# A block-sparse layer with a LoRA gate on one core: mask products a tile later, the second query ahead of a weight product, fills and mask products of the folds in other places

## The chip, the core and the metric

The kernel runs on one core of one Trainium2 chip. A core has five engines with a queue of instructions each: TensorE (PE in the profile; its weight loads are listed as PEld), VectorE (DVE), ScalarE (ACT), GpSimd (POOL) and SyncE (SP), which here issues loads and stores. Engines work side by side and meet at semaphores. Transfers between the chip's memory (HBM) and the core's SBUF are asked for by SP, ACT or POOL and carried by 16 DMA engines. Sums of matmuls are gathered in PSUM. The metric is the device time of one launch in microseconds (us); each kernel is run several times and the median is given.

## What is computed

```python
x  = L0_attn_data                              # [2, 1024, 1024]
xn = layernorm(x)
bm = mask.reshape(32, 32, 32, 32).sum(axis=(1, 3)) > 0     # 32 x 32 blocks
s  = einsum('bsk,nk->bsn', xn, weight * blocks(bm)) + bias
q      = einsum('bi,ki->bk', xn.mean(axis=1), Wq)
coeffs = softmax(einsum('bk,ek->be', q, keys) / sqrt(128))  # 8 experts
y  = xn @ W_org.T + einsum('be,bser,ero->bso', coeffs, xn @ lora_down, lora_up)
out = x + s * silu(y)
```

Everything is float32. The query q of a batch gives eight coefficients, so the gate's weights differ between the two batches: for each batch the kernel adds the scaled product of lora_down and lora_up into W_org once ("folding") and then multiplies by the sum.

## The kernel before

Each float32 operand is kept as two parts, a high part (a cast, on ScalarE) and a low part (what the cast lost, a subtraction on VectorE); a product is three matmuls, high by high, high by low, low by high. One tile of the output is 128 rows by 512 columns, summed over eight slices of 128 (`kt`), so 24 matmuls (lines 450, 453, 454). All of batch 0 is done in this way, in four stages of eight tiles (S and gate, two column halves each). Batch 1 runs after it in eight "units" of a Strassen scheme (line 1213), with seven sums of x for each slice group (`fill`, lines 1051 to 1063) and seven sums of weights (`unit_mask`, `unit_sum`, `unit_split`).

The order on TensorE, VectorE, ScalarE and GpSimd is that in which the program issues: the whole kernel is inside a manual schedule for these four. Only SP's order is the compiler's scheduler's.

The stages that the change touches:

- **Phase b** (`phase("y", 0, 0, y00, True, jobs_b)`, line 970 on). Eight tiles of batch 0's gate, each followed by one fold of the next weight half, `mix_jobs` (lines 873 to 883): `y_prep` loads a slice of lora_down (`ds`) and one of W_org (`wo`) and splits `ds` into `dhi` (ScalarE, L405) and `dlo` (VectorE, L406); `y_mul` is twelve matmuls into `psw` (L414 to L416); `y_sum` adds `psw` to `wo` on VectorE (L421). Before each tile `flush` issues what was put off: the sum of the last fold, the evacuation of the last tile, the low part. After the fold come the jobs of `jobs_b`. Among them are the block masks of quarters 2 and 3. A mask quarter is loaded in two parts; ScalarE sums each (L251); `mask_spread` makes a small operand `r` on VectorE (L261); `mask_apply_mm` is eight small matmuls with the constant `expand` (L271); `mask_apply_cp` copies the result into `m_sb` on VectorE (L278). `expand` lies in the first third of a buffer `misc`, which later takes loads of lora_up and of the x sums. Behind tile 3 `spread_stats` also turns batch 1's means and reciprocal deviations into rows: a transpose on TensorE (L927), a copy on ScalarE (L929), a store to HBM and two loads broadcast to all partitions on POOL's queue (L930, L934). `wide_a` and `wide_b` (lines 960 to 990) then normalize slices of x with these rows on VectorE (L962, L963) and form the sums (L968), which are stored to HBM.
- **Phase c** (`jobs_c`, line 997 on). Eight tiles of batch 0's gate, second half. Beside them `s_mul` (lines 295 to 303) loads a slice of the S weight, multiplies it by the mask on VectorE (L299) and casts it on ScalarE (L302), `s_lo` makes the low part (L307). Behind tile 5 stand the sums of batch 1's x (`steps[0]`, eight transposes, L322) and its query (`steps[1]`: two products with Wq on VectorE, L346, and `qb`, L350); in the middle of tile 6 stand the scores (`steps[2]`, a matmul that takes `qb`, L357); behind it the softmax and the scaling of lora_up.
- **The folds of batch 1** (lines 1132 to 1149). Five tiles of batch 0's second S half, with 4, 4, 3, 3 and 2 of the 16 folds behind them, and three more tiles after the folds. A fold n first issues `y_prep` of fold n+1, then the store of the last sum (`yu`, from ScalarE's queue), then the twelve matmuls, then the sum. Between folds stand the fills (a load of one x sum into one of three turns of `misc`, a cast on ScalarE, L1062, and a subtraction on VectorE, L1063) and the first six jobs of the first unit (`early`): two mask products of 1024 columns (L1091) and four sums of 512 (L1099). After fold 7 lora_up is scaled for the second half (`scale_up(1, 1, homes)`), with three of its four loads going into `misc`, in the turn behind the fills so far (L389, casts L392, low parts L393).

Of the kernel before, what the change touches and what calls it, by code (L numbers as in the profile page):

```python
# [32 lines left out]
def kernel(  # L33
# [99 lines left out]
    def nat_tile(dt=F32):  # L133
        k = turns[0] % 3
        turns[0] += 1
        v = raw_flat[:, k * D : (k + 1) * D]
        return v if dt == F32 else v.bitcast(dt)
# [107 lines left out]
    def mask_sum(qr, c, mt, eng, part=0):  # L245

        if qr not in msum:
            msum[qr] = small.tile([P, 2, 2], F32, name="s2")
        o = msum[qr][:, part, c : c + 1]
        if eng is nc.scalar:  # L250
            nc.scalar.activation(mt.bitcast(F32), mt, AF.Copy, accum_out=o)  # L251
        else:
            nc.vector.tensor_reduce(o, mt, AX.X, ALU.add)
# [5 lines left out]
    def mask_spread(qr):  # L259
        r4 = small.tile([P, 2, 4], BF16, name="r4")  # L260
        nc.vector.scalar_tensor_tensor(  # L261
            r4, msum[qr][:, 0, :].unsqueeze(2).to_broadcast([P, 2, 4]), 0.0,
            pick4.unsqueeze(1).to_broadcast([P, 2, 4]), ALU.is_gt, ALU.mult,
        )
        spread[qr] = r4

    def mask_apply_mm(qr):
        r4 = spread[qr]
        mp = ps_s.tile([P, NKT, 8], F32, name="mp", tag="ps_s")
        for kt in range(NKT):  # L270
            nc.tensor.matmul(  # L271
                mp[:, kt, :], lhsT=expand[:, kt * P : (kt + 1) * P],
                rhs=r4.rearrange("p a b -> p (a b)"), start=True, stop=True,
            )
        spread[qr] = mp

    def mask_apply_cp(qr):
        nc.vector.tensor_copy(m_sb[:, :, 8 * qr : 8 * (qr + 1)], spread[qr])  # L278

    def mask_part(qr, c, mt=None):  # L280
        if mt is None:
            mt = nat_tile(I32)
        else:
            mt = stage_l.tile([P, D], I32, name="mt", tag="ac", bufs=1)
        nc.sync.dma_start(mt, mask[2 * qr + c])
        mask_sum(qr, c, mt, nc.scalar)
        if c == 1:
            mask_spread(qr)
            mask_apply_mm(qr)
            mask_apply_cp(qr)  # L290

    def new_slot():
        return wpool.tile([P, NKT, 2, NH], F32R, name="slot", tag="w")
# [257 lines left out]
    J = lambda f, *a: (lambda: f(*a))  # L551
# [98 lines left out]
    with tc.manual_schedule(engines={mybir.EngineType.PE, mybir.EngineType.DVE, mybir.EngineType.Activation, mybir.EngineType.Pool}):  # L650
# [237 lines left out]
        def jobs_b(i):  # L888
            if i == 0:
                yield J(scale_up, 0, 1)  # L890
            yield J(mix_jobs, y01, 0, 1, i)
            yield J(store_out, 1)
            if i < 3:
                yield J(act_stats, 1 + i)
            for t in ((4,), (5, 6), (7,), (), (), (), (), ())[i]:
                yield J(nat_stats, t)
            yield from {
                2: [J(mask_part, 2, 0)], 3: [J(mask_part, 2, 1), J(spread_stats), J(mask_part, 3, 0, 1)],
                4: [J(mask_part, 3, 1, 1)],
            }.get(i, ())  # L900
            if i == 3:
                yield J(wide_load, 0, 0)
            if i == 4:
                yield J(wide_load, 0, 1)
                yield J(wide_a, 0)
            if i == 5:
                yield J(wide_b, 0)
                yield J(wide_load, 1, 0)
            if i == 6:
                yield J(wide_a, 1)  # L910
            if i == 7:
                yield J(wide_load, 1, 1)
# [63 lines left out]
        def wide_b(j):  # L976
# [12 lines left out]
            store_sums()  # L989

        phase("y", 0, 0, y00, True, jobs_b)


        s1 = new_slot()
        steps = coeffs(1)

        def jobs_c(i):
            if i < 2:
                yield J(store_out, 1 - i)

            if i < 6:
                yield J(s_mul, s1, 1, i)
            if i == 5:
                yield steps[0]
                yield steps[1]
            if i == 6:
                yield steps[3]
                yield J(scale_up, 1, 0, up_homes)
            if i == 5:
                yield J(s_mul, s1, 1, 6)  # L1010
                yield J(s_mul, s1, 1, 7)
                for kt in (5, 6, 7):
                    yield J(s_lo, s1, 1, kt)
            if i in (0, 2):
                yield J(wide_load, 2 + i // 2, 0)
                yield J(wide_load, 2 + i // 2, 1)
            if i < 5:
                yield J((wide_b, wide_a)[i % 2], 1 + (i + 1) // 2)
                yield J(s_lo, s1, 1, i)

        up_homes = [misc[:, 0, :]]
        split_at[(0, 1, 6)] = steps[2]
        phase("y", 0, 1, y01, False, jobs_c)


        folds = [(h, kt) for h in range(2) for kt in range(NKT)]

        def fold(n):
            h, kt = folds[n]
            if n + 1 < len(folds):  # L1030
                y_prep(1, *folds[n + 1])
            store_late()
            y_mul(1, h, kt)
            flush()
            y_sum(1, h, kt)
            ps, ws = staged.pop((1, h, kt))
            late_stores.append((
                yu[:, :, 2 * h + kt // 4, kt % 4, :].rearrange("u p n -> p u n"),
                ws.rearrange("p (u n) -> p u n", n=P),
            ))  # L1040
            if n == NKT - 1:
                homes = [misc[:, (len(spare) + k) % 3, :] for k in range(3)]
                spare.extend(homes)
                scale_up(1, 1, homes)
# [23 lines left out]
        def s_tile(i):  # L1068
            store_out()
            flush()  # L1070
            ps = gemm(0, i, s1)
            pending.append(J(final_evac, "s", 0, 1, i, ps))
# [6 lines left out]
        def unit_load(u, i):  # L1079
            kind, p = units[u]  # L1080
            src = wu[p] if kind == "s" else yu[p].rearrange("p a j n -> p (a j n)")
            c = slice(2 * i * NH, 2 * (i + 1) * NH)
            nc.sync.dma_start(raw_flat[:, c], src[:, c])
# [45 lines left out]
        def fills(j, n):  # L1129
            for _ in range(n):  # L1130
                fill(j, ORDER_X[filled[j]])
                filled[j] += 1

        for i, n in enumerate((4, 4, 3, 3, 2)):
            s_tile(i)
            for k in range(n):
                fold(done)
                done += 1
                if i < 3 and (i == 2 or k in (1, 2)):
                    fills(0, 1)  # L1140
                if i > 2 and (i == 4 or k):
                    fills(1, 1)
                if i in (2, 3):
                    early.pop(0)()
            if i == 0:
                unit_load(0, 0)
                unit_load(0, 1)
# [219 lines left out]
```

## Time and profile before

| what | value |
|---|---|
| median of 3 runs | 451.43 us (451.36 to 451.67) |
| the profiled execution, its own time | 452.2 us |
| its span, first to last instruction | 450.5 us |
| granted TensorE clock | 0.999 |
| TensorE busy | 440.4 us (98%) |
| VectorE busy | 288.9 us (64%) |
| ScalarE busy | 175.7 us (39%) |
| mean traffic to and from HBM | 200 GB/s |

The profile is one execution. Its page gives busy time by engine, the span in 40 slices, the chain of work that ended last, and the costliest groups of instructions. The trace behind it can be asked for the waits of an engine (who waited for whom, us in total, times, longest), for a timeline (start in us from the span's start, duration, engine, line, operation, output <- inputs, times, and in brackets the idle time of the engine before it with what ended it) and for more. A matmul of 512 columns is listed with 0.39 us because its end is modelled and it overlaps the next one; the distance between two starts, 0.227 us, is what it takes.

### The profile page before, as it was taken

Reading aid. Unit: us, or ns where it says so; the run is one execution under the profiler, and the core shown is the slowest. Engines: PE = TensorE matmul, PEld = TensorE weight load, DVE = VectorE, ACT = ScalarE, POOL = GpSimd, SP = SyncE. Lnnn points to the kernel's source line nnn. Section 1 sums busy time; section 2 is a strip of 40 time slices with the busy share of each in tenths; the row PEclk is TensorE's granted clock in tenths of the full one; section 3 lists DMA queues with packets and bytes.
Section 4 is the critical chain, followed back from the end, with each engine's and each line's share of the span. In section 5 each row is a group of like instructions: output and inputs, shape, how many; then the busy total and the mean of one; then the engine's idle time right before and its main releaser. Section 6 shows DMA issues by size and latency. Waiting matters only on the chain.

```text
span 450.5 us, 5791 instructions
## 1 busy us (share of the span) xinstructions
PE 440.4 (98%) x2058; PEld 363.7 (81%) x2058; DVE 288.9 (64%) x478; ACT 175.7 (39%) x291; POOL 76.4 (17%) x93
## 2 busy tenths in 40 slices
PE   8999999999999999999999999999999999999996
PEld 6789888888878888878887788887888888888885
DVE  6989777766627778864466667487456294365625
ACT  4676535454731222233233135067344322441520
POOL 3774210002220313120000000110020030002000
PEclk9999999999999999999999999999999999999999
DMA  8995306677896889896978987865183146218103
GB/s 280 391 353 198 134 25 210 235 240 224 252 291 184 262 259 331 275 346 192 283 211 284 317 244 226 244 178 187 39 187 140 47 112 170 93 23 218 42 1 116
DMA packets 47741, 90.58 MB, mean 201 GB/s; under 512 B 4816, under 2 KB 15328, under 8 KB 47712
## 3 DMA queue, kind: packets, MB, share of 16 engines
q1 hardware_dynamic: 30624, 66.08, 43.7%
q0 software_dynamic: 6624, 16.26, 15.5%
q10 hardware_dynamic: 10464, 7.87, 5.3%
q8 instruction: 16, 0.26, 0.2%
q14 instruction: 13, 0.11, 0.1%
HBM read 70.26 MB, written 19.93 MB: 200 GB/s over the span
## 4 chain that ended last, share of the span: by engine, by line
PE 68%; DVE 11%; DMA 11%; issue 6%; ACT 3%; POOL 1%; SPq 0%; ACTq 0%; DVEq 0%; POOLq 0%
PE acc_ps L1213 25%; PE py L1213 10%; PE acc_ps L454 7%; PE acc_ps L450 7%; PE acc_ps L453 7%; PE psw L416 4%; PE psw L414 4%; PE psw L415 4%; DMA ws<-in_wT_dram 3%; DMA stash<-in_x_dram 2%; DMA yu<-wo 2%; DVE st L145 1%; DVE slot L591 1%; DMA raw<-in_x_dram 1%; DMA raw<-in_mask_dram 1%
## 5 line engine op out<-in xcount | busy, mean ns | idle before, releaser
L1213 PE MATMUL acc_ps<-xw,ow 128*128 128x512 f32 (+1 forms) x492 | 113.3, 387 | 0.0
L1213 PEld LDWEIGHTS acc_ps<-xw,ow 128*128 128x128 f32 x492 | 91.0, 188 | 19.8 <-ACT acc_ps L1273 0.4
L450 PE MATMUL acc_ps<-slot,xgrp 128*128 128x512 f32 (+1 forms) x288 | 106.5, 370 | 0.1
L454 PE MATMUL acc_ps<-slot,xgrp 128*128 128x512 f32 (+1 forms) x288 | 105.7, 367 | 0.7 <-DVE xgrp L603 0.7
L453 PE MATMUL acc_ps<-slot,xgrp 128*128 128x512 f32 (+1 forms) x288 | 105.7, 367 | 0.6 <-DVE slot L591 0.4
L453 PEld LDWEIGHTS acc_ps<-slot,xgrp 128*128 128x128 f32 x288 | 54.4, 189 | 10.7 <-DVE slot L591 2.1
L454 PEld LDWEIGHTS acc_ps<-slot,xgrp 128*128 128x128 f32 x288 | 54.2, 188 | 10.2 <-DVE xgrp L603 1.1
L450 PEld LDWEIGHTS acc_ps<-slot,xgrp 128*128 128x128 f32 x288 | 54.3, 188 | 9.1 <-DVE stash L466 0.3
L416 PE MATMUL psw<-cut,dlo 128*128 128x512 f32 x128 | 50.0, 390 | 1.2 <-DVE dlo L406 1.2
L414 PE MATMUL psw<-cut,dhi 128*128 128x512 f32 x128 | 50.0, 390 | 0.0
L415 PE MATMUL psw<-cut,dhi 128*128 128x512 f32 x128 | 49.8, 389 | 0.0
L1213 PE MATMUL py<-xw,ow 128*128 128x512 f32 x192 | 46.8, 392 | 0.0
L1213 PEld LDWEIGHTS py<-xw,ow 128*128 128x128 f32 x192 | 36.1, 188 | 7.9
L1106 DVE TENSOR_TENSOR ow<-raw,ow 128x1024 fp32r<-128x1024 f32 (+1 forms) x32 | 34.5, 1088 | 10.9 <-ACT ow L1105 10.9
L405 ACT CAST dhi<-ds 128x512 fp32r<-128x512 f32 x32 | 19.7, 617 | 39.3 <-DMA ds<-in_down_dram 17.0
L502 POOL DMA_DIRECT2D stash<-in_x_dram x16 | 14.4, 898 | 121.5 <-DVE stash L499 121.5
L421 DVE TENSOR_TENSOR wo<-wo,psw 128x512 f32<-128x512 f32 x32 | 21.9, 685 | 16.3 <-PE psw L416 16.0
L1105 ACT CAST ow<-raw 128x1024 fp32r<-128x1024 f32 (+1 forms) x32 | 29.4, 941 | 2.2 <-DVE wo L421 1.6
L416 PEld LDWEIGHTS psw<-cut,dlo 128*128 128x128 f32 x128 | 24.0, 188 | 6.6 <-DVE dlo L406 1.6
L414 PEld LDWEIGHTS psw<-cut,dhi 128*128 128x128 f32 x128 | 24.0, 188 | 5.3 <-ACT dhi L405 0.4
L415 PEld LDWEIGHTS psw<-cut,dhi 128*128 128x128 f32 x128 | 24.1, 188 | 5.0
L1196 POOL DMA_DIRECT2D gate<-in_xT_dram x12 | 10.5, 909 | 94.2 <-DVE gate L1190 68.8
(180 smaller groups left out, 480.5 us busy)
## 6 DMA issues: line engine op xcount, KB each, us to landing
ds<-in_down_dram SPq DMA_DIRECT2D x32, 256.0 KB, 3.6
wo<-in_worgT_dram SPq DMA_DIRECT2D x32, 256.0 KB, 3.8
raw<-in_x_dram SPq DMA_DIRECT2D x11, 512.0 KB, 4.8
stash<-in_x_dram POOLq DMA_DIRECT2D x16, 256.0 KB, 5.2
raw<-in_wu_dram SPq DMA_DIRECT2D x8, 512.0 KB, 4.9
yu<-wo ACTq DMA_DIRECT2D x16, 256.0 KB, 4.9
raw<-yu SPq DMA_DIRECT2D x8, 512.0 KB, 3.6
out_dram<-stash ACTq DMA_DIRECT2D x14, 256.0 KB, 3.9
```

The costliest lines, as they stand in the source:

```text
L405: nc.scalar.copy(dhi, ds)
L414: nc.tensor.matmul(ps, lhsT=dhi[:, c, :], rhs=u[c][:, 0, :], start=c == 0, stop=False)
L415: nc.tensor.matmul(ps, lhsT=dhi[:, c, :], rhs=u[c][:, 1, :], start=False, stop=False)
L416: nc.tensor.matmul(ps, lhsT=dlo[:, c, :], rhs=u[c][:, 0, :], start=False, stop=c == 3)
L421: nc.vector.tensor_tensor(ws, ws, ps, ALU.add)
L450: nc.tensor.matmul(ps, lhsT=xs[:, kt, 0, cols], rhs=w[:, kt, 0, wc], start=kt == 0, stop=False)
L453: nc.tensor.matmul(ps, lhsT=xs[:, kt, 0, cols], rhs=w[:, kt, 1, wc], start=False, stop=False)
L454: nc.tensor.matmul(ps, lhsT=xs[:, kt, 1, cols], rhs=w[:, kt, 0, wc], start=False, stop=kt == NKT - 1)
L502: nc.gpsimd.dma_start(res, x[at], accum_op=ALU.add)
L1105: nc.scalar.copy(o[:, a:b, 0], raw[:, a:b])
L1106: nc.vector.tensor_tensor(o[:, a:b, 1], raw[:, a:b], o[:, a:b, 0].bitcast(F32), ALU.subtract)
L1213: nc.tensor.matmul(ps, lhsT=o[:, a, wl, j, :], rhs=xw[j][:, m, xl, cols], start=start and j == 0 and k == 0, stop=j == 3 and k == 2, skip_ ...
```

## The change

Three edits, none of which adds or drops an instruction. The line numbers of the profile are those of the kernel before; from line 290 on, those of the changed kernel are one higher.

1. The masks of quarters 2 and 3 are no longer spread, multiplied and copied right behind the issue of their second load. `mask_apply` does it one tile later: quarter 2 behind tile 4 (ahead of the second load of quarter 3), quarter 3 behind tile 5.
2. In phase c, behind tile 5, the sums and the query of batch 1 are issued ahead of the sixth S weight's `s_mul`, not behind it.
3. In the folds of batch 1 the fills of the first tile of x move from folds 1, 2, 5, 6, 8, 9, 10 (counted from 0) to folds 1, 2, 3, 4, 5, 9, 10; the mask products and sums of the first unit move from folds 8 to 13 to folds 8, 11, 12, 13, 14, 15. The turns of `misc` that lora_up takes after fold 7 follow the number of fills so far, which is now five and was four.

On SP the scheduler puts the first S weight's load ahead of a lora_up load, and the loads of x sums and lora_up between the folds in the new order.

```diff
@@ mask_part @@
         nc.sync.dma_start(mt, mask[2 * qr + c])
         mask_sum(qr, c, mt, nc.scalar)
-        if c == 1:
-            mask_spread(qr)
-            mask_apply_mm(qr)
-            mask_apply_cp(qr)
+
+    def mask_apply(qr):
+        mask_spread(qr)
+        mask_apply_mm(qr)
+        mask_apply_cp(qr)
@@ jobs_b @@
                 2: [J(mask_part, 2, 0)], 3: [J(mask_part, 2, 1), J(spread_stats), J(mask_part, 3, 0, 1)],
-                4: [J(mask_part, 3, 1, 1)],
+                4: [J(mask_apply, 2), J(mask_part, 3, 1, 1)], 5: [J(mask_apply, 3)],
             }.get(i, ())
@@ jobs_c @@
-            if i < 6:
-                yield J(s_mul, s1, 1, i)
             if i == 5:
                 yield steps[0]
                 yield steps[1]
+            if i < 6:
+                yield J(s_mul, s1, 1, i)
@@ the folds of batch 1 @@
                 fold(done)
                 done += 1
-                if i < 3 and (i == 2 or k in (1, 2)):
+                if i < 3 and k in ((1, 2, 3), (0, 1), (1, 2))[i]:
                     fills(0, 1)
                 if i > 2 and (i == 4 or k):
                     fills(1, 1)
-                if i in (2, 3):
+                if (i, k) in ((2, 0), (3, 0), (3, 1), (3, 2), (4, 0), (4, 1)):
                     early.pop(0)()
```

## The prediction

> **What bounds the kernel now.** The page comes first: TensorE is busy nearly all the span, and the later half of the chain of waits is matmuls alone. So only TensorE's own idle time can be won back. The waits of TensorE after that, which list where it stood still for another engine.
>
> ```profile
> PE 440.4 (98%) x2058; PEld 363.7 (81%) x2058; DVE 288.9 (64%) x478; ACT 175.7 (39%) x291; POOL 76.4 (17%) x93
> ```
> ```profile
> PE psw L416 <- DVE dlo L406: 1.2, 1, 1.2
> ...
> PE sp L357 <- DVE qb L350: 0.9, 1, 0.9
> ...
> PE mp L271 <- DVE r L261: 0.5, 1, 0.5
> ```
>
> Three of these single waits lie after the ramp (before 60 us), and each edit aims at one. I then read TensorE's timeline for their true width. A matmul of 512 columns starts 0.227 us after the one before it (122.14, 122.37, 122.59 us); anything more between two starts is loss. From 60 us to the end only three places lose over 0.35 us:
>
> ```profile
> 131.35 0.39 PE L416 MATMUL psw<-cut,dlo 128*128 128x512 f32 x1
> 132.28 0.35 PE L271 MATMUL mp<-r,misc 128*128 128x8 bf16 x8 [0.54 <-DVE r L261]
> 132.50 0.48 PE L450 MATMUL acc_ps<-slot,xgrp 128*128 128x512 f32 x1
> 132.81 0.40 PE L453 MATMUL acc_ps<-slot,xgrp 128*128 128x512 f32 x1
> ...
> 140.78 0.39 PE L450 MATMUL acc_ps<-slot,xgrp 128*128 128x512 f32 x1
> ...
> 193.18 0.39 PE L454 MATMUL acc_ps<-slot,xgrp 128*128 128x512 f32 x1
> 194.50 0.36 PE L357 MATMUL sp<-keys_sb,qb 128*128 128x8 f32 x2 [0.94 <-DVE qb L350]
> ...
> 247.06 0.40 PE L415 MATMUL psw<-cut,dhi 128*128 128x512 f32 x1
> 248.67 0.50 PE L416 MATMUL psw<-cut,dlo 128*128 128x512 f32 x1 [1.21 <-DVE dlo L406]
> ```
>
> The reader sees a mask product at 131.6 (quarter 3), scores at 193.4, and fold 10 (counted from 0) at 247.0. After the first of them the matmuls are back at full pace at 132.81, as if tile 5 had begun at 132.81 - 0.227 = 132.58; the products before ended at 131.35 + 0.227 = 131.58, so the first place costs 132.58 - 131.58 = 1.00 us. Last, VectorE's timeline around tile 5, since it decides what the first edit does:
>
> ```profile
> 132.06 0.17 DVE L261 SCALAR_TENSOR_TENSOR r<-s,pick 128x8 bf16<-128x8 f32 x1 [4.26 <-ACT mt L251]
> ...
> 135.75 1.23 DVE L962 TENSOR_TENSOR ac<-ac,raw 128x1024 f32<-128x1024 f32 x1 [2.85 <-DMA raw<-rows_d]
> 137.53 1.23 DVE L963 SCALAR_TENSOR_TENSOR ac<-ac,raw 128x1024 f32<-128x1024 f32 x1 [0.55 <-DMA raw<-rows_d]
> ...
> 138.68 0.68 DVE L421 TENSOR_TENSOR wo<-wo,psw 128x512 f32<-128x512 f32 x1
> ...
> 142.46 1.22 DVE L962 TENSOR_TENSOR raw<-raw 128x1024 f32<-128x1024 f32 x1
> ```
>
> VectorE is held at 135.75 and 137.53 us by the broadcast of batch 1's mean and rstd rows, a transfer, and so runs late: dlo (L406), just ahead of the last line shown, starts at 141.85, when TensorE is already into tile 6, which began at 140.78.
>
> **What the Trainium skill says.** "TensorE: Matmul & The Clock Gate", section "Architectural detail: the array is 16× 32×32, not 1× 128×128", has VectorE and ScalarE as strict first-in-first-out queues, and its section "The mechanism" says matmuls neither start nor end out of program order. The trace agrees: TensorE idled 0.94 us ahead of the scores though the rest of tile 6 depended on nothing late. "DMA: Bandwidth & Descriptors", section "Anatomy of one DMA — SWDGE (gpsimd) path", says a wait is served by the issuing sequencer before dispatch; so a load that waits holds those behind it on SP. The trace shows SP's loads of wo (L402) held up to 3.8 us each by stores of yu. Durations below are the trace's.
>
> **Edit 1, the mask products one tile later.** The order of the built program shows the eight matmuls of quarter 2 moved from behind tile 3 to behind tile 4, and those of quarter 3 from behind tile 4 to behind tile 5, each with its r (L261) ahead and its copy (L278) behind on VectorE. Nothing is added or dropped. After tile 3: the last matmul at 122.59 would be followed at 122.82; the mask block starts 123.06, the row transpose 123.26, and tile 4 at an effective 123.59 - 0.227 = 123.36. With the transpose alone (0.10 of that) it is 122.92: gain 0.44. After tile 4: r of quarter 2 has its sums since 122.8, so no wait is left, and the block costs its own 132.58 - 132.28 = 0.30, say 0.35 with its start: gain 1.00 - 0.35 = 0.65. TensorE now ends the products of tile 5 at 140.78 - 0.44 - 0.65 = 139.69.
>
> There it meets quarter 3's block, whose r stands on VectorE behind dlo, where L962 was at 142.46. The sums for it are ready at 132.0; but VectorE reaches it only after L962, L963, L421, the evacuation and dlo, all behind the row broadcast. I move that chain forward by 0.42 (the transpose starts at 122.84 instead of 123.26, and ScalarE and POOL wait only for it), and by an estimated 0.2, from 0 to 0.5, because a 256 KB load of up weights issued at 132.67 beside the broadcast now stands behind quarter 3's product. So r at 142.46 - 0.62 = 141.84, the block 0.22 later (132.06 to 132.28), tile 6 at 141.84 + 0.22 + 0.30 = 142.36 against 140.78: **+1.58** net, a wait of some 2.4 us in place of 0.54. Bounds: -0.8 (VectorE there in time) to +2.2 (nothing moved forward). Behind the waiting matmuls stand tile 6 and all TensorE work. VectorE's copy waits about 0.5 for the products, delaying the sums of the wide tiles by that; no matmul needs them before 189.78 (the xrow transposes, ready since 187.2). On SP the first S weight load goes ahead of the up load; the S weight, issued near 142, is used at 162, the up load later.
>
> **Edit 2, the query ahead of the sixth S weight.** Before, the S product at 192.12 waited 1.71 us for its weight, and the query's L346 and L350 followed, 192.73 to 194.35. Now they start once the last low part ends, 190.4, with xrow there since about 190.5: qb at 190.5 + 1.62 = 192.1, ahead of 193.41, when TensorE wants it. If TensorE is late by edit 1, xrow is late alike, and 1.62 still fits into the half tile (12 x 0.227 = 2.72). The gap 193.18 to 194.50 holds 1.32 - 0.227 = 1.09 of loss: **-1.08**, bounds -1.1 and 0. The weight product then starts at most 2 us later; its slot is read 10 us later.
>
> **Edit 3, fills and mask products over the folds.** In fold 10 dlo came at 247.93, needed by 247.0. Ahead of it on VectorE stood a fill (xw, 246.18, which waited for its cast and so for a transfer) and the first mask product (246.79, 1.22); on ScalarE dhi stood at 246.06 behind the fill's cast.
>
> ```profile
> 246.18 0.69 DVE L1063 TENSOR_TENSOR xw<-misc,xw 128x512 fp32r<-128x512 f32 x1 [0.77 <-ACT xw L1062]
> 246.79 1.22 DVE L1091 TENSOR_TENSOR raw<-raw,m_sb 128x1024 f32<-128x1024 f32 x1
> 247.93 0.69 DVE L406 TENSOR_TENSOR dlo<-ds,dhi 128x512 fp32r<-128x512 f32 x1
> ```
>
> The seven fills of the first tile stood in folds 1, 2, 5, 6, 8, 9, 10 and now stand in 1 to 5, 9, 10; so in fold 8 the mask product alone is left ahead of that dlo. The up loads into misc follow one fill earlier in their ring, so the cuts (L393), which ended at 242.9, end near 239.5. Then: fold 8's sum after its products at 243.83, to 244.5; the mask product to 245.7; dlo 245.7 to 246.4, 0.6 ahead of need. dhi needs ds, issued 240.84 behind a yu store and landing, at the median 3.6 us, at 244.4; cast to 245.1. The loss here is 0.17 + 0.10 + 1.38 + 0.10 (starts at 246.73, 247.06, 248.67, 249.00): **-1.75**, bounds -1.75 and 0. What is late next: the second mask product stands ahead of fold 13's dlo, 261.2 to 261.9 against 262.55; covered by 0.6. The last two sums run beside the last folds; their splits are wanted at 292.1.
>
> **Sum.** 1.58 - 1.08 - 1.75 = -1.25 us. The profiled execution took 452.2 us (span 450.5, 1.7 around it), 0.8 above the median of the runs; I take the difference to the median: 451.43 - 1.25 = **450.2**.
>
> **Rivals.** *Quarter 3 isn't waited for.* If VectorE reaches r by 139.7 us, edit 1 gains 1.09 less 0.3 for its own block, and the sum is -0.8 - 1.08 - 1.75 = -3.6: 447.8. For it speaks that the sums are ready 7 us earlier; against it VectorE's strict order behind the broadcast. *The fold stays late.* The mask product still stands ahead of dlo; if ds lands after 245.7 (it waits for a store that took 7 us), 1.0 to 1.75 is not won: 451.2 to 452.0, about no change. *Slower: the row broadcast lands later.* Before, VectorE's lateness there cost TensorE nothing; now every microsecond of it is one of TensorE. It landed at 137.5; 0.42 is mine to move. With a landing past 139.1, 2.2 us later than I take it, the sum passes +0.9; at 139.5 it is about +1.35: 452.8. POOL's queue or the stores beside it could do that; nothing in the trace before does.
>
> **How the numbers follow.** A measurement can tell 0.2% here, 0.9 us: faster is below 450.53, slower above 452.33. The forecast has 0.60, of that 0.42 below 450.53, 0.16 within, 0.02 above (its spread is the landing of the broadcast, about 0.6, and part of edit 3). Quarter 3 in time 0.10, faster; the fold late 0.20, same; the broadcast late 0.10, slower. Together 0.52, 0.36, 0.12. The range 449.3 to 451.7 leaves out the first rival and the last, 0.2.
>
> **What would show it.** After: TensorE waits for r at L271 once, over 1.5 us, near 140 us, and the wait for qb is gone; no wait for dlo over 0.3; VectorE meets its broadcast near 135. If TensorE's wait for r is under 0.5, edit 1's step is wrong; if a wait for dlo or dhi over 1 us stands near 247, edit 3's is.

## The result, and the profile after

| what | before | after |
|---|---|---|
| median of 22 runs each, side by side | 451.55 us (450.1 to 452.71) | 453.77 us (450.64 to 456.82) |
| ratio, with 95% interval | | 1.0052 (1.0036 to 1.0068) |
| the profiled execution, its own time | 452.2 us | 452.61 us |
| its span | 450.5 us | 450.9 us |
| its granted TensorE clock | 0.999 | 0.995 |

The changed kernel is slower: 2.3 us, with 1.6 to 3.1 in the interval, where 1.25 less was forecast. It also scatters more than before, and with the clock: of its 22 runs, six had a granted clock of 0.998 or more, and took 451.4 us on average; the other sixteen, at 0.991 to 0.996, took 454.8.

In the page after, TensorE's share of busy time is again 98%; what is new stands in the row of the clock, where one slice of 40 shows 8, the one from 135.3 to 146.5 us.

```profile
PE 441.5 (98%) x2058; PEld 365.3 (81%) x2058; DVE 289.3 (64%) x478; ACT 175.8 (39%) x291; POOL 76.5 (17%) x93
...
PEclk9999999999998999999999999999999999999999
```

The waits of TensorE after: the ones for `qb` and `dlo` are gone, as meant, and the one for `r` is four times as long.

```profile
PE mp L271 <- DVE r L261: 2.1, 1, 2.1
PE warm L673 <- DVE ones_r L93: 1.1, 1, 1.1
PE pt L206 <- ACT acc L163: 0.9, 1, 0.9
PE acc_ps L455 <- DVE xgrp L604: 0.7, 2, 0.5
PE acc_ps L454 <- DVE slot L592: 0.6, 3, 0.2
```

VectorE's timeline after, at the place the forecast names. `r` is the last of a row that begins with the two passes over the broadcast rows (L963, L964).

```profile
135.41 1.23 DVE L963 TENSOR_TENSOR ac<-ac,raw 128x1024 f32<-128x1024 f32 x1 [3.26 <-DMA raw<-rows_d]
137.10 1.23 DVE L964 SCALAR_TENSOR_TENSOR ac<-ac,raw 128x1024 f32<-128x1024 f32 x1 [0.47 <-DMA raw<-rows_d]
...
138.25 0.68 DVE L422 TENSOR_TENSOR wo<-wo,psw 128x512 f32<-128x512 f32 x1
140.21 0.69 DVE L500 TENSOR_TENSOR stash<-stash,mine 128x512 f32<-128x512 f32 x1 [1.27 <-ACT mine L476]
140.82 0.68 DVE L433 TENSOR_TENSOR slot<-wo,slot 128x512 fp32r<-128x512 f32 x1
141.42 0.69 DVE L407 TENSOR_TENSOR dlo<-ds,dhi 128x512 fp32r<-128x512 f32 x1
142.03 0.16 DVE L261 SCALAR_TENSOR_TENSOR r<-s,pick 128x8 bf16<-128x8 f32 x1
```

And TensorE's timeline after. Look at the starts of the 512-column matmuls, not at their durations: up to 139.78 and from 146.62 on they lie 0.227 us apart, from 143.34 to 146.32 they lie 0.43 apart.

```profile
139.78 0.39 PE L417 MATMUL psw<-cut,dlo 128*128 128x512 f32 x1
142.24 0.34 PE L271 MATMUL mp<-r,misc 128*128 128x8 bf16 x8 [2.07 <-DVE r L261]
142.44 0.47 PE L451 MATMUL acc_ps<-slot,xgrp 128*128 128x512 f32 x1
142.75 0.39 PE L454 MATMUL acc_ps<-slot,xgrp 128*128 128x512 f32 x1
142.98 0.56 PE L455 MATMUL acc_ps<-slot,xgrp 128*128 128x512 f32 x1
143.34 0.63 PE L451 MATMUL acc_ps<-slot,xgrp 128*128 128x512 f32 x1
143.76 0.63 PE L454 MATMUL acc_ps<-slot,xgrp 128*128 128x512 f32 x1
...
146.32 0.46 PE L454 MATMUL acc_ps<-slot,xgrp 128*128 128x512 f32 x1
146.62 0.40 PE L455 MATMUL acc_ps<-slot,xgrp 128*128 128x512 f32 x1
```

The table by stage shows why. Its columns are the busy share of TensorE, its weight loads, VectorE, ScalarE and GpSimd (with the number of instructions), then the granted clock, the DMA share and GB/s. From 141 to 142 us TensorE does nothing; from 143 us on it is busy without a break, at half its clock.

```profile
141.00:142.00 1.00, 0.00 (x0) 0.00 (x0) 1.00 (x2) 0.00 (x0) 0.67 (x1) 1.00 0.00 0
142.00:143.00 1.00, 0.76 (x11) 0.68 (x11) 0.57 (x4) 0.00 (x0) 0.19 (x1) 1.00 0.39 90
143.00:144.00 1.00, 1.00 (x4) 0.81 (x3) 0.97 (x1) 0.00 (x0) 0.00 (x0) 0.52 0.87 176
144.00:145.00 1.00, 1.00 (x3) 0.76 (x3) 0.99 (x1) 0.00 (x0) 0.00 (x0) 0.50 1.13 215
145.00:146.00 1.00, 1.00 (x4) 0.76 (x3) 0.96 (x4) 0.00 (x0) 0.00 (x0) 0.50 0.93 291
146.00:147.00 1.00, 1.00 (x5) 0.82 (x4) 1.00 (x2) 0.00 (x0) 0.00 (x0) 0.77 0.08 21
```

The two mixed rows date the change. A row reads 0.52 when the clock was at half for 0.96 of its microsecond, which puts the fall at 143.04 us; 0.77 in the same way puts the rise at 146.46. So the clock was at half for 3.42 us. As an estimate, one such stretch lowers the mean clock of a whole run by half of 3.42/451, to 0.996, and two lower it to 0.992. Of the sixteen runs with a lowered clock ten lie at 0.995 or 0.996 and six at 0.991 or 0.992.

In this pair of traces the account is even: from the first matmul after 58 us to the last one, before took 388.38 us and after 388.41. Gone are 0.9 at the mask products, 1.1 at the scores, 1.75 at fold 10; new are 2.2 of waiting for `r` and 1.6 at half clock (eleven starts from 142.98 to 146.85 took 3.87 us, ten pitches are 2.27). "TensorE: Matmul & The Clock Gate" of the Trainium skill describes such a fall in its section "What's actually happening" (half the clock after an idle window of about 3.4 us, free-running), and its section "HAM oscillation — how this bites in real kernels" warns of idle gaps longer than that. The half clock agrees with the trace, and so does the length of the window; the length of the idle time doesn't: 2.07 us of waiting were enough here.

**Theory A** after this: edit 1 lets TensorE stand idle for `r`, and the idle time itself takes the clock down for some 3 us more, in most runs. **Theory B**: the clock is an accident of these runs or of this chip, and the loss lies in edits 2 and 3, which on average win less than in the one trace or give it back elsewhere. **Theory C** is the third rival of the prediction: the row broadcast is what TensorE waits for.

### The profile page after: what moved, and what is told of

It reads as the page before. It is cut to its first block, busy times and chain, and to the rows that moved or that the text cites. A ratio compares the mean times of both kernels' runs of the same rounds, so it can differ in the third digit from the quotient of the medians.

```text
span 450.9 us, 5789 instructions
## 1 busy us (share of the span) xinstructions
PE 441.5 (98%) x2058; PEld 365.3 (81%) x2058; DVE 289.3 (64%) x478; ACT 175.8 (39%) x291; POOL 76.5 (17%) x93
## 4 chain that ended last, share of the span: by engine, by line
PE 91%; DVE 5%; DMA 2%; ACT 1%; issue 1%; POOL 0%; SPq 0%; ACTq 0%; DVEq 0%
PE acc_ps L1214 25%; PE acc_ps L455 12%; PE acc_ps L451 12%; PE acc_ps L454 12%; PE py L1214 10%; PE psw L417 6%; PE psw L415 6%; PE psw L416 6%; DMA raw<-rows_d 2%; DVE slot L592 1%; DVE ramp L583 1%; DMA acc<-in_x_dram 1%; PE warm L673 1%; DVE st L145 1%; DVE xgrp L604 0%
## 5 line engine op out<-in xcount | busy, mean ns | idle before, releaser
L407 DVE TENSOR_TENSOR dlo<-ds,dhi 128x512 fp32r<-128x512 f32 x32 | 22.0, 687 | 9.5 <-ACT dhi L406 9.4
```

The lines of the kernel that those rows point to most:

```text
L407: nc.vector.tensor_tensor(dlo, ds, dhi.bitcast(F32), ALU.subtract)
```

## The experiments

Every ratio below is to the kernel before, run beside it on the same chip, with its 95% interval. Microseconds behind a ratio are the ratio less 1, times 451.4. The expectations, quoted as they stood before each run, name their own theories and rivals anew each time; the A, B and C of the text outside them are the three above.

**Edits 2 and 3 without edit 1.** Back to before in:

```diff
-                4: [J(mask_apply, 2), J(mask_part, 3, 1, 1)], 5: [J(mask_apply, 3)],
+                4: [J(mask_part, 3, 1, 1)],
```

with spread, products and copy again behind each quarter's second load.

> Edits 2 and 3 without edit 1. Theory (edit 1 alone carries the loss: TensorE waits over 2 us for r behind tile 5, and its granted clock then falls to half for a while): the waits of 1.09 us for qb and 1.75 us for dlo are gone and nothing comes in their place, so 451.5 - 2.8 = 448.7 us, granted clock 0.999 in every run. Rival (the moved fills and mask products slow the kernel or spread its times, by transfers that land at other moments): 451 to 453 us, with times as far apart as those of the changed kernel.

Measured: 450.7 us, ratio 1.0003 (0.9982 to 1.0024), all 14 clocks 0.998 or more. Without edit 1 the clock fell in none of these runs: that is for A. (In the kernel before, run beside the experiments, 15 of 165 runs are at 0.996, and with edit 2 or edit 3 alone 2 of 36 lie below 0.998; what idle time stands behind those no trace shows.) But the two edits alone win 0 on average, at best 0.8, though the profiled execution of this kernel (span 447.5) shows none of the waits they aimed at. That part is for B.

**Edit 1 alone.** The diff of `mask_part` and `jobs_b`, with the orders of phase c and of the folds as before.

> Edit 1 alone. Theory: the wait for r behind tile 5 is there with some 2.1 to 2.4 us, tile 6 starts 1.6 us late, the wait for qb is swallowed by it (-1.1), the wait for dlo in fold 10 stays, and the clock falls in most runs, worth 2.0 us on average (1 less the mean clock of the changed kernel's runs, times its span): 451.5 + 1.6 - 1.1 + 2.0 = 454.0 us, runs spread over 4 us or more, clock 0.991 to 1.0. Rival (the loss comes from edits 2 and 3): 451.5 us or less, clock 0.999.

Measured: 454.93 us, ratio 1.0083 (1.0054 to 1.0112); six of eight clocks below 0.998. In its trace TensorE waited 4.1 us for `r`, twice as long, because the second broadcast row landed only at 139.13:

```profile
139.74 0.39 PE L417 MATMUL psw<-cut,dlo 128*128 128x512 f32 x1
144.26 0.35 PE L271 MATMUL mp<-r,misc 128*128 128x8 bf16 x8 [4.13 <-DVE r L261]
144.47 0.77 PE L451 MATMUL acc_ps<-slot,xgrp 128*128 128x512 f32 x1
145.05 0.63 PE L454 MATMUL acc_ps<-slot,xgrp 128*128 128x512 f32 x1
...
149.74 0.42 PE L451 MATMUL acc_ps<-slot,xgrp 128*128 128x512 f32 x1
```
```profile
142.00:143.00 1.00, 0.00 (x0) 0.00 (x0) 0.76 (x2) 0.71 (x2) 0.00 (x0) 0.97 0.70 262
...
149.00:150.00 1.00, 1.00 (x5) 0.76 (x4) 1.00 (x3) 0.00 (x0) 0.43 (x1) 0.61 0.03 10
```

The reader sees the half pitch at once, for 5.3 us, about 2.5 us lost. By the mixed rows the clock fell at 142.94, in the middle of the wait, and rose at 149.78: 6.84 us, twice the 3.42 of the changed kernel. Edit 1 carries the whole loss.

**The idle time filled.** Ten matmuls of ones (512 columns, 2.27 us, their sums read by nothing) stand on TensorE ahead of quarter 3's products; `r` comes as late as in the changed kernel.

```diff
+            for _ in range(fill):
+                nc.tensor.matmul(
+                    whole, lhsT=ones_r, rhs=ones_r.unsqueeze(1).to_broadcast([P, 4, P]), start=True, stop=True
+                )
...
-        mask_apply_mm(qr)
+        mask_apply_mm(qr, 10 if qr == 3 else 0)
```

> All three edits, and ten matmuls of 512 columns on constants, whose sums nothing reads, ahead of quarter 3's mask block: TensorE computes for 2.27 us where it idled. The wait for r stays as long, only its idle time is filled. Theory (idle time, not lateness, makes the clock fall): clock 0.998 or more in every run, and the changed kernel's time less its 2.0 us of clock: 451.8 us. Rival (the clock falls by chance, or the time is lost elsewhere): still 453 to 454 us with runs at 0.991 to 0.996.

Measured: 451.68 us, ratio 1.0018 (1.0004 to 1.0033), all 22 clocks 0.998 or more. In its trace `r` came at 142.00, as in the changed kernel (142.03), and tile 6 ran at full pace from there on:

```profile
140.28 2.43 PE L272 MATMUL mp<-ones_r 128*128 128x512 f32 x10
142.55 0.35 PE L279 MATMUL mp<-r,misc 128*128 128x8 bf16 x8
142.76 0.48 PE L459 MATMUL acc_ps<-slot,xgrp 128*128 128x512 f32 x1
143.09 0.39 PE L462 MATMUL acc_ps<-slot,xgrp 128*128 128x512 f32 x1
143.31 0.40 PE L463 MATMUL acc_ps<-slot,xgrp 128*128 128x512 f32 x1
143.55 0.40 PE L459 MATMUL acc_ps<-slot,xgrp 128*128 128x512 f32 x1
```

Ten useless matmuls more, and the kernel is faster than the changed one by a ratio of 1.0052 - 1.0018, 1.5 us (about 1 either way). Here late work doesn't take the clock down; an idle TensorE does.

**Half the filling.** The same with five matmuls, 1.13 us.

```diff
-        mask_apply_mm(qr, 10 if qr == 3 else 0)
+        mask_apply_mm(qr, 5 if qr == 3 else 0)
```

> The changed kernel with five further matmuls of 512 columns (1.13 us, their sums are read by nothing) ahead of quarter 3's mask products: of an idle time of 2.1 to 4.1 us before r, 1.0 to 3.0 stay; r itself comes when it came. Theory A (the clock falls when an idle time of some 2 us or more is seen): part of the runs fall, fewer than the 15 of 22 of the changed kernel and later than there; median 451.7 to 452.5, ratio 1.002 to 1.003. Rival B (any idle time of about 1 us at this place suffices): the clocks are as in the changed kernel, 0.991 to 0.996 in most runs, ratio 1.004 to 1.006. Rival C (it takes over 3 us): no run below 0.998, as with ten fillers, ratio 1.001 to 1.002.

Measured: 452.61 us, ratio 1.0034 (1.0017 to 1.0051), between the two and a little above what its theory A gave; 8 of 22 clocks below 0.998 (16 of 22 with no filling, none with ten). In its trace 2.22 us of waiting were left (the broadcast was at 138.44), and 3.1 us at half clock followed:

```profile
140.06 1.30 PE L272 MATMUL mp<-ones_r 128*128 128x512 f32 x5
143.58 0.36 PE L279 MATMUL mp<-r,misc 128*128 128x8 bf16 x8 [2.22 <-DVE r L261]
143.79 0.77 PE L459 MATMUL acc_ps<-slot,xgrp 128*128 128x512 f32 x1
144.37 0.63 PE L462 MATMUL acc_ps<-slot,xgrp 128*128 128x512 f32 x1
```

**`r` a tile earlier.** All three edits, but `r` of quarter 3 is issued behind tile 4, ahead of the passes over the broadcast rows; products and copy stay behind tile 5. Run twice, on two chips.

```diff
-                4: [J(mask_apply, 2), J(mask_part, 3, 1, 1)], 5: [J(mask_apply, 3)],
+                4: [J(mask_apply, 2), J(mask_part, 3, 1, 1), J(mask_spread, 3)], 5: [J(mask_apply_mm, 3), J(mask_apply_cp, 3)],
```

> All three edits, but quarter 3's r is made on VectorE where it was before, behind tile 4 and ahead of the wide tile's L963; only its eight matmuls and the copy stay one tile later. Theory (r waits behind the row broadcast in VectorE's queue): TensorE has no wait for r over 0.3 us, edit 1 then gains about 0.8, and the sum is 451.5 - 0.8 - 1.1 - 1.75 = 447.9 us, clock 0.999. Rival (the matmuls of quarter 3 are late for another reason, such as their PSUM buffer or the sums from ScalarE): a wait of over 1 us stays at L271 and the time stays above 450.

> All three edits with r of quarter 3 issued a tile earlier than its products, a second time. Theory A (the loss of the changed kernel is the wait for r and the clock after it, and nothing else): ratio 0.997 as in the first run, within 0.0015, all clocks 0.998 or more. Rival B (the first run was a lucky chip or set of runs): ratio 0.999 or more.

Measured: 449.7 us, ratio 0.9974 (0.9956 to 0.9991), then 450.37 us, ratio 0.9976 (0.9958 to 0.9994); clocks 0.998 or more in 29 of 30 runs. VectorE waits 1.8 to 1.9 us for quarter 3's sums where it waited for the broadcast anyway, and TensorE no more for `r`. The waits of TensorE in the second run, all before 60 us:

```profile
PE pt L206 <- ACT acc L163: 1.4, 1, 1.4
PE warm L673 <- DVE ones_r L93: 1.1, 1, 1.1
PE acc_ps L455 <- DVE xgrp L604: 0.7, 2, 0.5
PE acc_ps L454 <- DVE slot L592: 0.6, 3, 0.2
```

This is the version that beats both kernels: over both runs (ratio 0.9975) 1.1 us ahead of before, 3.5 ahead of the changed one. It falls short of the 447.9 expected.

**`r` between the broadcast and the rest of VectorE's queue.** As the changed kernel, but `r` stands right behind L964, ahead of the sum of the fold, the evacuation and `dlo`.

```diff
                 yield J(wide_load, 0, 1)
                 yield J(wide_a, 0)
+                yield J(mask_spread, 3)
...
-                4: [J(mask_apply, 2), J(mask_part, 3, 1, 1)], 5: [J(mask_apply, 3)],
+                4: [J(mask_apply, 2), J(mask_part, 3, 1, 1)], 5: [J(mask_apply_mm, 3), J(mask_apply_cp, 3)],
```

> The changed kernel with r of quarter 3 issued on VectorE right behind the last pass over the broadcast rows (L965), ahead of the sum of the fold, the evacuation of tile 5 and dlo; the mask products stay behind tile 5. In the traces so far that pass started at 137.1 to 139.1 us, so r comes at 138.3 to 140.3 against 139.4 to 139.8, when TensorE wants it. Theory A (r is late because of all that stands ahead of it on VectorE, the broadcast being only the first 60%, and the clock falls after the long idle time): a wait of 0 to 0.9 us, all clocks 0.998 or more, median some 450.0, ratio to before about 0.997 to 0.999. Rival B (the broadcast itself is what TensorE waits for, often landing past 139 us): waits of over 1.5 us stay, some runs with a clock of 0.992 to 0.996, ratio over 1.001.

Measured: 450.48 us, ratio 0.9979 (0.9959 to 0.9999), 19 of 22 clocks 0.998 or more (of the runs of before beside it, 62 of 67). `r` came at 138.19, and TensorE went on at 139.77 without a wait:

```profile
138.19 0.17 DVE L261 SCALAR_TENSOR_TENSOR r<-s,pick 128x8 bf16<-128x8 f32 x1
```
```profile
139.77 0.35 PE L271 MATMUL mp<-r,misc 128*128 128x8 bf16 x8
```

The broadcast was the earliest of all traces here (second row read from 137.04), so it is the 22 runs that decide: the broadcast is the lesser part, and theory C falls. What makes `r` late is the other work behind it, 3.8 us in the changed kernel's trace, from 138.25 to 142.03, 1.27 of which is VectorE itself waiting for ScalarE's half of an evacuation (L476).

**Edit 1 alone with `r` early.** The same line of `jobs_b` as in the version that wins, edits 2 and 3 undone.

> Edit 1 alone with r of quarter 3 issued behind tile 4 already (products and copy behind tile 5), edits 2 and 3 undone. What moving the products alone is worth, with no wait for r. Theory A (edit 1 would have brought the 0.8 us of the prediction's first rival, less what varies): 450.3 to 450.6 on a chip where before has 451.1 to 451.4, ratio about 0.998, all clocks 0.998 or more; waits for qb and dlo as in the kernel before. Rival B (the mask block behind tile 4 cost nothing on average, since its wait varies): ratio 0.999 to 1.001.

Measured: 451.63 us, ratio 1.0014 (0.9993 to 1.0035), 12 of 14 clocks 0.998 or more: on the side of its rival B. Without its wait edit 1 moves nothing that can be told, at best 0.3 us.

**Edit 2 alone, edit 3 alone, the kernel before once more, the changed kernel once more.** Four kernels for theory B, on one chip; the diffs of the first two are those of the change.

> Edit 2 alone. Theory A (the wait for qb is in every run as in the one traced): 1.1 us faster than before, 450.0 to 450.2 beside 451.1 to 451.3. Theory B (that wait is the lateness of a transfer in the one traced execution, and mostly shorter): 0 to 0.5 us faster; the trace shows no wait for qb.

> Edit 3 alone. Theory A (the wait for dlo in fold 10 is in every run as in the one traced): 1.75 us faster than before, about 449.5. Theory B (it depends on how late a transfer lands in that execution): 0 to 1 us faster, with runs as far apart as those of the kernel before.

> The kernel before, unchanged: a second traced execution and the distance that two equal kernels show. Theory A: the waits of TensorE for qb (0.9 us) and dlo (1.2 us) are there again within 0.3 us. Theory B: one or both differ by over 0.5 us, and the whole differs by as much. Ratio 1.000 within 0.002 in both.

> The changed kernel, unchanged: a second traced execution. Theory: TensorE waits for r behind tile 5 again, by 2 to 4 us according to when the row broadcast lands, and the clock falls behind it for one or two stretches of 3.4 us or not at all; over the runs the time goes up by about 0.45 us for each 0.001 of mean clock, and what is left at full clock lies within 1 us of the kernel before. Rival (the drop of the clock stood in that one execution by chance): no drop behind tile 5 in this trace, or one in another place.

Measured: edit 2 alone 450.39 us, 0.9989 (0.9974 to 1.0005). Edit 3 alone 450.33 us, 0.9986 (0.9964 to 1.0008). Before against itself 450.91 us, 0.9988 (0.9964 to 1.0011). The two edits can't be told from the kernel before run against itself. The changed kernel again: 454.27 us, 1.0049 (1.0029 to 1.0068), 15 of 22 clocks below 0.998, a wait of 3.7 us for `r` in its trace. The second trace of the kernel before is what tells most. These are its losses on TensorE's timeline:

```profile
123.90 0.34 PE L271 MATMUL mp<-r,misc 128*128 128x8 bf16 x8 [0.69 <-DVE r L261]
...
162.64 0.50 PE L450 MATMUL acc_ps<-slot,xgrp 128*128 128x512 f32 x1 [0.46 <-ACT slot L424]
...
195.68 0.36 PE L357 MATMUL sp<-keys_sb,qb 128*128 128x8 f32 x2 [0.73 <-DVE qb L350]
```

The mask wait stands behind tile 3 and not behind tile 4; a wait at 162 us is there that the first trace didn't have; at fold 10 only 0.34 us is lost, not 1.75. In sum this execution lost as much as the first: 388.0 us from the first matmul after 58 us to the last, against 388.4. And in edit 3's own trace 0.9 us appears where no other trace had more than 0.7, in the first unit of batch 1:

```profile
308.29 0.96 PE L1213 MATMUL acc_ps<-xw,ow 128*128 128x512 f32 x3 [0.92 <-ACT acc_ps L1273]
```

ScalarE's copy (L1273) stood there behind the casts of fills (L1062) that waited for loads of x sums, and behind a cast (L1105).

## Why the prediction was wrong

The forecast was -1.25 us: wins of 0.44 + 0.65 + 1.08 + 1.75 = 3.92, less 2.67 for TensorE's stop at quarter 3 (139.69 to 142.36). The runs gave +2.35: wins of 1.13 (both runs with an early `r`), less 3.48 for the stop (the changed kernel against those). Every sign that the prediction named came true in the trace after (one wait for `r` of over 1.5 us near 140 us, none for `qb` or `dlo`, the broadcast met at 135.41), but no sign looked at the clock or at a second execution.

- **The place of the new stop** was right: TensorE waits once for `r`, behind the row broadcast in VectorE's order. `r` was forecast for 141.84 and came at 142.03, tile 6 for 142.36 and came at 142.44 + (142.75 - 142.44 - 0.227) = 142.52. The first rival, quarter 3 in time, fell by this.
- **One step that failed is "tile 6 at 141.84 + 0.22 + 0.30 = 142.36 against 140.78: +1.58 net"**: it ends the price of the stop where the waiting ends. In four traces tile 6 then ran at half clock for 3.1 to 5.3 us, and 1.4 to 2.5 us were lost by it. On average over runs the clock is worth 1.5 us (the changed kernel against ten fillers), the waiting 1.9 (ten fillers against early `r`), each within about 1 us. The page that the prediction cites for the order of queues also treats the clock, as said above; the sum had no term for it.
- **The size of the wait** varies more than the 0.6 us given for it: 2.1, 3.7 and 4.1 us in three traces, as the second row was read from 137.10, 138.34 and 139.13 on. In the second trace of the kernel before it was 139.01, so it lands late without the change, too. That is the mechanism of the slower rival, and it adds to the loss; but the clock fell at 137.10 already, well short of its 139.1, so it doesn't decide.
- **Edits 2 and 3** did what their steps say. After, `qb` ended at 195.41, 1.35 us ahead of the scores (forecast 1.3), and fold 10's `dlo` at 248.67, 0.55 ahead of its first use at 249.22 (forecast 0.6). **The other step that failed, and the larger error, is "1.58 - 1.08 - 1.75 = -1.25 us"**: it takes one execution's losses for those of all. That execution took 452.2 us, and the kernel before runs from 449 to 455. Where the old order stood and no stop came before, four traces lost 1.09, 0.89, 0.99 and 0.51 us at the scores; at fold 10 the five with the old order lost 1.75, 0.34, 0.38, 0.53 and 1.03. So it is above all fold 10 that the one trace overstated. A wait at L1273 took back 0.9 in one trace. Edits 2 and 3 together, at 1.0003 (0.9982 to 1.0024), exclude the -2.83 forecast for them; 0.8 is the most that agrees.
- **Edit 1's wins**, 1.09, were such waits too: in the five traces with the masks as before, 0.95, 0.85, 1.09, 0.65 and 0.46 us were lost ahead of the two quarters' products together. Without that loss and with an early `r`, edit 1 alone still wins 0.3 at best. Its trace lost 1.2 us near 162, where the first trace of the kernel before lost nothing and the second 1.1.

Of the 3.6 us between forecast and result, then, 2.8 are wins that didn't come and 0.8 is the price of the stop, each within about 1 us.

**What stays open.** The three edits with an early `r` gave -1.1 us in two runs, edits 2 and 3 alone 0, edit 1 with an early `r` alone +0.6; the intervals (0.8 to 1.0 us either way) allow that these simply add up only if all three values lie far out in theirs. That a wait removed by one edit shows as the next late one until all are gone would explain it, and the second trace of the kernel before, with other waits and the same sum, fits this; the runs don't show it. Nor does a trace show what the longer runs of a kernel with hardly a wait lose: the four such executions that were profiled took 449.0 to 449.8 us, the medians of their kernels are 449.7 to 450.7. Two of the four were the fastest or second fastest of their kernel's runs, while both profiled executions of the kernel before lay above its median, so traces set side by side show more gain than the runs do. And why about a third of the changed kernel's runs kept their clock is open. A shorter wait would do; so would a wait of some 2 us that is split between two stretches of 3.42 us, if the clock is judged by such stretches. No execution that kept it was profiled.

## What to carry to other kernels

Before an operation is moved later on TensorE, find its operand's producer in the order of *its* engine and move that one separately: the products may go a tile later, the small `r` must stay ahead of whatever waits for a transfer. Price a stop of TensorE of 2 us or more with the clock after it, here about 1.5 us (0.5 to 2.5) on average on top of the waiting. And a single wait of one trace is no prize until a second execution shows it at the same place with the same size: here the wait for `qb` came back with 0.7 us for 0.9, the one for `dlo` hardly at all.

## What the runs showed of the hardware

- TensorE's clock halves (pitch 0.43 in place of 0.227 us) after waits of 2.07, 2.22, 3.71 and 4.13 us. By the mixed rows of the table by stage the half clock lasts 3.4, 3.4, 6.8 and 6.8 us, one or two of the same stretch. After the shortest wait it began 0.8 us after work had resumed; in the other three it began during the wait. When it began, TensorE had been idle for 2.07, 2.02, 2.5 and 2.8 us of the 3.4 us before. The longest wait that no fall followed in any trace was 1.43 us (near 7 us, edit 3 alone).
- The granted clock of the whole run tells of it: over its 44 runs the changed kernel's time follows 451.5 us plus 0.53 for each 0.001 that the clock lies below 1. Of that, 0.45 is the clock itself (451 times 0.001).
- Useless matmuls in an idle stretch won 1.5 us here, though they do nothing but keep the engine busy.
- The same broadcast of rows isn't equally late in two executions of one and the same kernel: the second row was read from 137.53 and from 139.01 us on in the kernel before, from 137.10 and 138.34 in the changed one.
